# Sixty instead of fifty-six single-row gather tiles in a graph-attention layer

## Chip, cores and metric

One Trainium2 chip, one core of it. The metric is the device time of one execution in microseconds (us), median of three timed executions, lower is better. A profiled execution stands beside them; its trace gives every number that is not a timed one.

## What is computed

A graph layer over N = 6250 nodes and E = 206250 edges (sorted by receiver), 128 features in 8 heads of 16, all float32:

```
w   = silu(edge_feats @ rad_W1 + rad_b1) @ rad_W2 + rad_b2
    + silu(chi_scalar @ sph_W1 + sph_b1) @ sph_W2 + sph_b2     # per edge
q   = (x @ Wq)[receivers];  k = (x @ Wk)[senders];  v = (x @ Wv)[senders]
alpha = (q * w * k).sum(head) / sqrt(16) * cutoffs             # 8 numbers per edge
out = segment_sum(alpha * v, receivers) / 16
return layernorm(x + out)
```

## The kernel before

**Stages.** A first stage (some 65 us) makes the table kv_tab in device memory: one row of 1 KB per node, k and v side by side. Then one long loop runs over the edges. 128 edges are a tile, four tiles a *quad*, four quads a *group*; there are 403 quads, taken in an order that swaps the two middle ones of a group. The loop has one *slot* per quad, and in slot i the engines are at different quads: TensorE (PE) makes the hidden layer of quad i+2 (L533), brings q to the edges of quad i+1 (L542) and weighs quad i+1 (L580); ScalarE (ACT) takes the two silus of quad i+2 (L563) and a copy out of PSUM; VectorE (DVE) multiplies quad i+1 by the k of its senders (L593) and ends quad i (L601 to L620: product, sum over heads, scale, messages). PE sums the messages by receiver with one-hot matrices (L632), and per group the totals are normalized and written (L690 to L749).

**How the sender rows come.** GpSimd (POOL) issues one indirect DMA per tile (L136, `gather`), 128 rows of kv_tab by the indices of the tile, into a ring of 16 quads. It is 14 quads ahead of the loop: the gathers of quad i+14 wait for the matmuls of quad i (`gathers`). The quads 0 to 7 need no gather (their rows are made from gathered x in the first stage).

**Single rows.** In 56 of the quads (`row_quads`) the fourth tile is not gathered. Its 128 rows are fetched by 128 plain DMAs of one row each (L203, `load_rows`), 64 issued by SyncE (SP) and 64 by ACT, into a buffer named wide. The row addresses are in a table at_i, and an engine loads them into its registers some at a time (`ROW_UNITS`; L198), before the issues. The places of these quads are `row_at`: evenly between ROW_FIRST and ROW_LAST. The issues for tile k are spread over the slots from row_at[k-1] - ROW_LEAD + 1 to row_at[k] - ROW_LEAD; in each slot SP's come at the end of its program for the slot, ACT's behind its second silu, but for two (ROW_CARRY) that are kept for the next slot and put one before and one behind the PSUM copy, between the two silus (`copies`, `next_rows`). In a row quad DVE's multiply and its messages are two instructions each, three tiles from kv and one from wide (`kv_parts`).

**The end.** The last quads 400 to 402 are summed without the receivers' 32-wide one-hots: three wide one-hots (L639 to L643 on DVE, `wide_one_hots`) are made in slots 392, 394 and 396 and scaled by ACT (L650, four instructions) in slots 393, 395 and 397. They share the three buffers named wide with the single-row tiles. The totals of four groups are kept in y0 (two buffers) until they are written.

**Order.** The order on each engine is the program's own (the schedule is by hand); what waits is in order behind what waits before it on its engine or queue.

Of the kernel before, what the change touches and what calls it, by code (L numbers as in the profile page):

```python
# [12 lines left out]
F32 = mybir.dt.float32  # L13
# [8 lines left out]
SP = mybir.EngineType.SP  # L22
ACT = mybir.EngineType.Activation
WAIT = mybir.DependencyInfo(mybir.DependencyClass.Sync, mybir.DependencyReason.DATA)

P = 128
N = 6250
D = 128
# [5 lines left out]
QT = 4  # L34
# [10 lines left out]
LB = 4  # L45
# [1 line left out]
XQ = 8  # L47
MSGS = 10
RING = 16
ROW_TILES = 56  # L50
ROW_FIRST = 20
ROW_LAST = 392
ROW_LEAD = 8
ROW_ACT = 64
ROW_CARRY = 2
ROW_UNITS = {SP: 32, ACT: 32}
XU = 4
WRITE_LAG = 3
READY_LAG = 2
# [10 lines left out]
def gnn_kernel(ctx, tc, x, src, dst, weight, edges, rad_W1, rad_b1, rad_W2, rad_b2,  # L70
# [26 lines left out]
    src_x = const.tile([P, math.ceil(XQ / NQ) * GT], I32, name="src_x")  # L97
    at_i = const.tile([ROW_TILES, P], I32, name="at_i")
    scale = const.tile([P, NT], F32, name="scale")
# [23 lines left out]
    gp = ctx.enter_context(tc.tile_pool(name="group", bufs=2))  # L123
# [8 lines left out]
    def quad_of(name, bufs, width=D):  # L132
        return ep.tile([P, QT, width], F32, name=name, bufs=bufs)
# [8 lines left out]
    order = [g * NQ + j for g in range(NG) for j in (0, 2, 1, 3) if g * NQ + j < QUADS]  # L142
    row_at = [ROW_FIRST + (n + 1) * (ROW_LAST - ROW_FIRST) // ROW_TILES for n in range(ROW_TILES)]
    row_quads = {order[i] for i in row_at}
# [22 lines left out]
    feats_of, relb_of, act_of, kv_of, hot_of, hotT_of, x_of, q_of, msg_of = ({} for _ in range(9))  # L167
    po_of, part_of, to_of, tot_of, xT_of, y0_of, kq_of, pick_of, pq_of, pw_of = ({} for _ in range(10))
# [16 lines left out]
    def load_rows(i):  # L185

        k = next((k for k in range(ROW_TILES) if i <= row_at[k] - ROW_LEAD), None)
        start = None if k is None else (row_at[k - 1] if k else ROW_FIRST) - ROW_LEAD + 1
        if k is None or i < start:
            return next_rows(ACT, owed[ACT])  # L190
        q = order[row_at[k]]
        slots = row_at[k] - ROW_LEAD + 1 - start
        table = kv_tab.bitcast(U8).rearrange("(o n) b -> o (n b)", o=1)

        def rows_by(engine, name, a, b):
            for e in range(a, b, ROW_UNITS[name]):
                m = min(ROW_UNITS[name], b - e)
                rows = nc.values_load_multi_w_load_instructions(  # L198
                    at_i[k:k + 1, e:e + m], engines=(name,), min_val=0,
                    max_val=(N - 1) * ROW_BYTES,  # L200
                    skip_runtime_bounds_check_because="senders are nodes")[1]
                for p, r in zip(range(e, e + m), rows):
                    yield lambda p=p, r=r: signalled(engine.dma_start(  # L203
                        row_of[q][p:p + 1, 0, :].bitcast(U8), table[:, ds(r, ROW_BYTES)]))
# [7 lines left out]

        n = P - ROW_ACT
        if i == start:
            row_of[q] = quad_of("wide", 3, P)[:, :2, :].rearrange("p t d -> p (t d)")[:, None, :]
            rows_left[SP].append(rows_by(nc.sync, SP, 0, n))
            rows_left[ACT].append(rows_by(nc.scalar, ACT, n, P))
        for engine, m in ((SP, n), (ACT, ROW_ACT)):
            a, b = (math.ceil(m * j / slots) for j in (i - start, i - start + 1))
# [99 lines left out]
    with tc.tile_pool(name="nodes", bufs=1) as nodes, \  # L319
# [76 lines left out]

        rows_f = nodes.tile([P, ROW_TILES], F32, name="rows_f")

# [6 lines left out]
        def turn_rows():  # L405
            pt = nps.tile([P, QT, P], F32, name="pt", bufs=3)
            nc.tensor.transpose(pt[:ROW_TILES, 0, :], rows_f, ident)
            nc.vector.tensor_copy(at_i, pt[:ROW_TILES, 0, :])

# [117 lines left out]
    with tc.tile_pool(name="ps", bufs=1, space=PSUM) as pp, tc.tile_pool(name="loop", bufs=1) as lp:  # L527
# [108 lines left out]
        def wide_one_hots(q):  # L636

            t = slice(q * QT, (q + 1) * QT)
            d = gp.tile([P, QT], F32, name="d", bufs=NQ)  # L639
            nc.vector.tensor_copy(d, dst_i[:, t])  # L640
            nc.vector.tensor_scalar(d, d, gb[:, q // NQ:q // NQ + 1], None, op0=OP.subtract)
            hot_of[q, "wide"] = quad_of("wide", 3, P)
            nc.vector.tensor_tensor(hot_of[q, "wide"], d[:, :, None].to_broadcast([P, QT, P]),  # L643
                                    colp[:, None, :].to_broadcast([P, QT, P]), op=OP.is_equal)

# [33 lines left out]
        def first_of(g):  # L679

            return max(g - (g - (NG - LB)) % LB, 0)

        def moments(g, total, adder=nc.vector, added=False):
            first = first_of(g)
            if g == first:
                y0_of[g] = (gp.tile([P, LB, D], F32, name="y0"), gp.tile([P, LB, 2], F32, name="mv"))
            y0, mv = y0_of[first]
            k = g - first
            if not added:
                adder.tensor_tensor(y0[:, k, :], total, x_of[g], op=OP.add)  # L690
            st = gp.tile([P, 6], F32, name="st")
            nc.vector.bn_stats(st, total if added else y0[:, k, :])
            nc.vector.bn_aggr(mv[:, k, :], st)
# [45 lines left out]
        def statistics(g):  # L739
            moments(g, tot_of[g])  # L740
            if g < NG - LB and first_of(g + 1) > g:
                inverse_roots(first_of(g), g + 1)
# [42 lines left out]
        for g in range(NG - 1):  # L785
            for slot, j in enumerate((0, 2, 1, 3)):
                q = g * NQ + j
# [56 lines left out]
                if g == NG - 3 and slot in (0, 2):  # L844
                    wide_one_hots(order[slot // 2 - 3])
                if g == NG - 2 and slot == 0:
                    wide_one_hots(order[-1])
                    n = nc.values_load(general, min_val=0, max_val=1)
                    place(g)
                    place(NG - 1)  # L850
# [34 lines left out]
        for t in range(QT):  # L885
            sum_wide(b, t)
        moments(g - 2, tot_of[g - 2], nc.gpsimd)
        multiply(c, mark)
        moments(g - 1, tot_of[g - 1], nc.gpsimd)
        sd = roots(g - 2, g)  # L890
        normalize(g - 2, g, sd)
# [10 lines left out]
        ys, mv = y0_of[first_of(g)]  # L902
# [162 lines left out]
```

## Time and profile before

| | us |
|---|---|
| timed executions | 1966.3, 1967.48, 1971.83 (median 1967.48) |
| profiled execution, its own time | 1966.43 |
| its span, first to last instruction | 1964.3 |
| mean granted PE clock | 0.942 |
| POOL busy | 1476.0 |
| PE busy | 1770.4 |
| DVE busy | 1516.8 |
| ACT busy (without its DMA issues and register loads) | 648.3 |
| gathers by POOL in the loop's ring | 1524 |
| single rows by SP, by ACT | 3584, 3584 |

A row of the waits names who waited, for what, the total in us, the number of waits and the longest. A row of the timeline has start, duration, engine, line, operation, result and sources, and in brackets the idle time of the engine before it and what ended it. A row of the windows has the stretch, its length, busy us and number of instructions, the granted PE clock, the busy share of the 16 DMA engines and GB/s. POOL's duration of a gather is the time to issue it; the rows land later.

### The profile page before, as it was taken

How to read it: one execution, taken by the hardware profiler on the slowest of the kernel's cores; microseconds unless marked ns; L12 is line 12 of the kernel's file. 1: busy time of each engine (PE TensorE's matmuls, PEld its weight loads, DVE VectorE, ACT ScalarE, POOL GpSimd, SP SyncE). 2: the span in 40 equal slices, each digit the busy share in tenths (PEclk: the TensorE clock that was granted, in tenths of full speed). 3: DMA queues.
4: the chain of work that ended last, by engine and by line, in shares of the span. 5: the costliest groups of instructions: out<-in, count | busy, mean ns of one | idle time of the engine just before them, and what ended most of it. 6: DMA issues, size and time to landing. Idle time of an engine off the chain costs nothing. (4 is left out here: it accounts for less than half of the span.)

```text
span 1964.3 us, 57621 instructions
## 1 busy us (share of the span) xinstructions
PE 1770.4 (90%) x15990; PEld 1480.0 (75%) x15990; DVE 1516.8 (77%) x3411; ACT 648.3 (33%) x1360; POOL 1476.0 (75%) x1566
## 2 busy tenths in 40 slices
PE   9899999799999888889999988989889988898898
PEld 7788777677877777777877777778777777777776
DVE  6788888688877687777787777877777777777787
ACT  3333333232433333332332333333323323333333
POOL 7777777777777777777777777777777777777775
PEclk9899999898989899989899899999998999999999
DMA  9555555555555555555555555555555555555553
GB/s 343 154 151 147 154 155 148 155 156 148 159 148 152 155 150 157 147 158 156 157 146 157 147 157 146 155 148 155 156 146 156 147 155 150 152 158 145 157 143 93
DMA packets 153253, 305.44 MB, mean 155 GB/s; under 512 B 40300, under 2 KB 87260, under 8 KB 152924
## 3 DMA queue, kind: packets, MB, share of 16 engines
q0 software_dynamic: 74176, 201.95, 36.7%
q1 hardware_dynamic: 70080, 95.67, 15.6%
q10 hardware_dynamic: 8668, 4.08, 1.0%
q8 instruction: 127, 2.08, 0.5%
q14 instruction: 202, 1.65, 0.3%
HBM read 288.10 MB, written 13.46 MB: 154 GB/s over the span
## 5 line engine op out<-in xcount | busy, mean ns | idle before, releaser
L136 POOL DMA_INDIRECT kv<-kv_tab,src_i x1524 | 1442.6, 947 | 465.0 <-issue 198.8
L563 ACT ACTIVATE act<-ph,b 128x512 f32<-128x512 f32 x806 | 553.3, 687 | 1259.5 <-PE pq L542 598.0
L580 PE MATMUL pw<-w,act 128*128 128x128 f32 x6448 | 881.4, 293 | 0.0
L580 PEld LDWEIGHTS pw<-w,act 128*128 128x128 f32 x6448 | 802.0, 203 | 96.3 <-issue 79.0
L533 PE MATMUL ph<-feats,w 32*128 32x512 f32 x1612 | 545.4, 670 | 58.5 <-ACT act L563 57.0
L542 PE MATMUL pq<-q,hotT 32*128 32x128 f32 x3224 | 487.6, 292 | 5.9 <-DVE kq L593 5.8
L593 DVE TENSOR_TENSOR kq<-pq,kv 128x512 f32<-128x512 f32 (+1 forms) x403 | 269.8, 669 | 249.1 <-DVEq L590 110.0
L542 PEld LDWEIGHTS pq<-q,hotT 32*128 32x128 f32 x3224 | 408.8, 195 | 19.7 <-DVE kq L593 15.5
L603 DVE TENSOR_REDUCE side<-kq 128x32 f32<-128x512 f32 x403 | 279.9, 695 | 43.6 <-DVE kq L601 1.4
L620 DVE TENSOR_TENSOR msg<-kv,side 128x512 f32<-128x512 f32 (+1 forms) x404 | 269.8, 668 | 43.5 <-PE pw L580 1.2
L533 PEld LDWEIGHTS ph<-feats,w 32*128 32x128 f32 x1612 | 154.0, 191 | 178.0 <-ACT act L563 115.6
L601 DVE TENSOR_TENSOR kq<-pw,kq 128x512 f32<-128x512 f32 x403 | 274.1, 680 | 0.6 <-PE pw L580 0.6
L575 PE MATMUL pw<-brow,onesb 3*128 3x512 bf16 x403 | 158.6, 393 | 0.6 <-DVE kq L601 0.6
L632 PE MATMUL po<-msg,hot 128*32 128x128 f32 x3200 | 156.6, 294 | 0.0
L673 PE MATMUL pq<-part,to 128*128 128x128 f32 x200 | 48.8, 330 | 95.6 <-DVE kq L593 93.2
L673 PEld LDWEIGHTS pq<-part,to 128*128 128x128 f32 x200 | 33.7, 212 | 105.1 <-DVE kq L593 90.2
L607 DVE TENSOR_TENSOR side<-side,scale 128x32 f32<-128x32 f32 x400 | 79.8, 200 | 42.3 <-DVE side L603 0.9
L632 PEld LDWEIGHTS po<-msg,hot 128*32 128x32 f32 x3200 | 73.1, 113 | 38.4 <-issue 4.6
L272 DVE TENSOR_TENSOR hotT<-relb,side 128x512 f32<-128x512 bf16 x101 | 68.7, 681 | 0.0
L277 DVE TENSOR_TENSOR hot<-rel,side 128x512 f32<-128x512 f32 x100 | 68.0, 680 | 0.0
L266 PE MATMUL pq<-wq,xT 128*128 128x128 f32 x200 | 41.6, 290 | 17.9 <-DVE kq L593 17.6
L690 DVE TENSOR_TENSOR y<-tot,x 128x128 f32<-128x128 f32 x98 | 28.2, 287 | 27.3 <-DMA out<-y 27.3
(121 smaller groups left out, 831.9 us busy)
## 6 DMA issues: line engine op xcount, KB each, us to landing
wide<-kv_tab SPq DMA_DIRECT2D x3584, 1.0 KB
wide<-kv_tab ACTq DMA_DIRECT2D x3584, 1.0 KB
feats<-in_edges SPq DMA_DIRECT2D x101, 512.0 KB
kv<-kv_tab,src_i POOLq DMA_INDIRECT x1524
relb<-rel_lin SPq DMA_DIRECT2D x101, 128.0 KB
x<-in_x SPq DMA_DIRECT2D x101, 64.0 KB
out<-y SPq DMA_DIRECT2D x101, 64.0 KB
kv_tab<-kv SPq DMA_DIRECT2D x12, 512.0 KB
```

Of the source, the lines that this page charges most:

```text
L136: return nc.gpsimd.indirect_dma_start(out=o, out_offset=None, in_=table, in_offset=bass.IndirectOffsetOnAxis(ap=index, axis=0))
L533: return nc.tensor.matmul(act_of[q, i], w1[r0:r0 + R, :], feats_of[g][r0:r0 + R, c0:c0 + EQ], start=True, stop=True)
L542: o = nc.tensor.matmul(pq_of[q][:, t, :], hotT_of[g][b, t * P:(t + 1) * P], q_of[g][b, :], start=True, stop=True)
L563: o = nc.scalar.activation(act, act_of[q, i], AF.Silu, bias=b1[:, i:i + 1])
L575: nc.tensor.matmul(pw, onesb, brow.rearrange("p t d -> p (t d)"), start=True, stop=False)
L580: o = nc.tensor.matmul(pw[:, t, :], act_of[q, i][:, t * P:(t + 1) * P], w2[:, i, :], start=False, stop=(t == QT - 1 and i == 1))
L593: o = nc.vector.tensor_tensor(kq_of[q][:, u, :], pq_of[q][:, u, :], kv[:, :, :D], op=OP.mult)
L601: nc.vector.tensor_tensor(m, pw_of[q][:, t, :], m, op=OP.mult)
L603: o = nc.vector.tensor_reduce(alpha, m.rearrange("p t (h e) -> p t h e", e=HD), AX.X, OP.add)
L620: o = nc.vector.tensor_tensor(msg_of[q][:, u, :].rearrange("p t (h e) -> p t h e", e=HD), kv[:, :, D:].rearrange("p t (h e) -> p t h e", e ...
L632: o = nc.tensor.matmul(po_of[g][j * W:(j + 1) * W, :], hot_of[g][:, j * QT + t, :], msg_of[g * NQ + j][:, t, :], start=(t == 0), stop=(t = ...
L673: nc.tensor.matmul(ph[:, :D], to[:n, 0, :], part[:n, :], start=True, stop=(g == 0))
```

## The change

There are 60 single-row quads, spread from 4 to 401 instead of from 20 to 392; they come every 6.617 instead of every 6.643 slots, the first is quad 10 (before: 26), the last 401 (before: 392). ACT issues 68 and SP 60 of the 128 rows. The issues of a tile end 5 instead of 8 slots ahead of its quad. ACT loads 24 addresses at a time: three loads a tile (24, 24, 20) instead of two of 32; SP has two, of 32 and 28. The wide one-hots of the end get three buffers of their own, and y0 has three buffers instead of two, both in the space that the first stage leaves free.

```
-ROW_TILES = 56
-ROW_FIRST = 20
-ROW_LAST = 392
-ROW_LEAD = 8
-ROW_ACT = 64
+ROW_TILES = 60
+ROW_FIRST = 4
+ROW_LAST = 401
+ROW_LEAD = 5
+ROW_ACT = 68
 ROW_CARRY = 2
-ROW_UNITS = {SP: 32, ACT: 32}
+ROW_UNITS = {SP: 32, ACT: 24}
...
-            hot_of[q, "wide"] = quad_of("wide", 3, P)
+            hot_of[q, "wide"] = lp.tile([P, QT, P], F32, name="hots", bufs=3)
...
-                y0_of[g] = (gp.tile([P, LB, D], F32, name="y0"), gp.tile([P, LB, 2], F32, name="mv"))
+                y0_of[g] = (lp.tile([P, LB, D], F32, name="y0", bufs=3), gp.tile([P, LB, 2], F32, name="mv"))
```

## The prediction

> **What bounds the kernel now.** I began with the page: who is busy, and who does the same thing most often. Then the waits, POOL first.
>
> ```profile
> span 1964.3 us, 57621 instructions
> L136 POOL DMA_INDIRECT kv<-kv_tab,src_i x1524 | 1442.6, 947 | 465.0 <-issue 198.8
> ```
>
> ```profile
> POOL kv L136 <- issue: 198.8, 652, 0.3
> POOL kv L136 <- PE pw L580: 182.3, 597, 0.3
> DVE kq L593 <- DVEq L590: 110.0, 69, 4.0
> DVE y L690 <- DMA out<-y: 27.3, 6, 9.3
> ```
>
> POOL never waits longer than 0.3 us before a gather: that is the step from one gather to the next, not a wait, whatever engine it is put down to. So POOL issues without a pause from the first gather to the last, while DVE stands 69 times in front of L590, where it waits for rows. The ends of that row of gathers in the timeline, and what DVE does behind it:
>
> ```profile
> 44.25 0.95 POOL L136 DMA_INDIRECT kv<-kv_tab,src_i  x1 [0.30 <-issue]
> ...
> 1950.56 0.95 POOL L136 DMA_INDIRECT kv<-kv_tab,src_i  x1 [0.30 <-issue]
> ...
> 1953.60 0.69 DVE L593 TENSOR_TENSOR kq<-pq,kv 128x512 f32<-128x512 f32 x1 [0.69 <-DVEq L590]
> ```
>
> (1950.56 - 44.25) / 1523 = **1.2517 us a gather**, start to start. POOL is the bound of the long middle; a gather that is left out there is worth 1.25 us.
>
> **From gather to multiply.** POOL's end is not DVE's start: the rows must land. Counting back from the last gather, 40 belong to quads 393 to 402, three to row quad 392, 24 to 386 to 391; so the last gather of 385 starts 67 steps before 1950.56 and that of 384 70 steps. For 395 it is 28 steps and for 396 it is 24. On DVE quad 385 is known by its split multiply.
>
> ```profile
> 1863.07 0.95 POOL L136 DMA_INDIRECT kv<-kv_tab,src_i  x1 [0.30 <-DVE side L607]
> 1866.82 0.95 POOL L136 DMA_INDIRECT kv<-kv_tab,src_i  x1 [0.30 <-issue]
> 1870.99 0.69 DVE L593 TENSOR_TENSOR kq<-pq,kv 128x512 f32<-128x512 f32 x1 [1.09 <-DVEq L590]
> 1875.04 0.56 DVE L593 TENSOR_TENSOR kq<-pq,kv 128x384 f32<-128x384 f32 x1
> 1875.52 0.28 DVE L593 TENSOR_TENSOR kq<-pq,wide 128x128 f32<-128x128 f32 x1
> ...
> 1915.55 0.94 POOL L136 DMA_INDIRECT kv<-kv_tab,src_i  x1 [0.30 <-issue]
> 1918.49 0.69 DVE L593 TENSOR_TENSOR kq<-pq,kv 128x512 f32<-128x512 f32 x1 [0.28 <-DVEq L590]
> 1920.56 0.94 POOL L136 DMA_INDIRECT kv<-kv_tab,src_i  x1 [0.30 <-issue]
> 1923.54 0.69 DVE L593 TENSOR_TENSOR kq<-pq,kv 128x512 f32<-128x512 f32 x1
> ```
>
> From the end of the last gather to the multiply: 1870.99 - 1864.02 = **6.97 us** for quad 384, waiting for rows to the last; 7.27 for 385; but 1918.49 - 1916.49 = 2.00 for 395 and 1923.54 - 1921.50 = **2.04 us** for 396. What lies between is the end of the single rows:
>
> ```profile
> L203 ACTq DMA_DIRECT2D wide<-kv_tab x3584: 227/228/788, 123.4 to 1878.9; - x200
> ```
>
> ```profile
> 1000.00:1500.00 500.00, 73.21 (x121) 0.94 0.54 153
> 1900.00:1924.00 24.00, 3.98 (x7) 1.00 0.38 108
> ```
>
> The last is issued at 1878.9, and the DMA engines' share falls from 0.54 to 0.38. While single rows are on their way a gather needs 5 us longer to land. A constant lag costs nothing in a loop; but where it ends the loop gets 5 us back, and before, that happened in time: quads 386 to 396 ran faster than POOL's step.
>
> **The change, part by part.** *POOL.* Four gathers fewer, 4 x 1.2517 = 5.0 us, at its last gather. At quad 396 it is three (59 of 60 row quads lie at or before 394, against all 56): its last gather ends 3.75 us earlier, at 1917.75. Nothing holds POOL back: the rows of the waits say so, and the first row quad takes one gather from a start where it waits for none.
>
> *The end of the rows.* The issues now run to slot 396, so quad 396 has a lag like 384's, not like 396's: 1917.75 + 6.97 = 1924.72 against 1923.54: **+1.2 us**. Bounds for the lag: 2.04 (the rows don't matter: -3.75 in all) and 7.27 (+1.5). I take 6.97, the quad as far from the last issue. The 5 us come back only in quads 398 to 402, and there they find no taker:
>
> ```profile
> DVE st L692 <- PE ph L654: 0.9, 1, 0.9
> DVE kq L593 <- DVEq L590: 0.7, 1, 0.7
> DVE kq L601 <- PE pw L580: 0.6, 1, 0.6
> ```
>
> These are DVE's longest waits from 1924 to the end: 2.2 us of 37, and for rows 0.7. From quad 396 on DVE works through (wide one-hots, inverse roots, the tail), and its start sets the end.
>
> *DVE.* Quad 401 becomes a row quad in that tail: 0.56 + 0.28 - 0.69 = 0.15 us, for the multiply and for the messages, **+0.3**. The other three stand where DVE waits for rows: nothing (0.9 us if it did not). The four added address columns before the loop, by this row
>
> ```profile
> 57.88 2.43 DVE L402 TENSOR_SCALAR rows_f<-src_i 128x1 f32<-128x1 int32 x39
> ```
>
> cost 4 x 0.06 us, with quads in stock: nothing.
>
> *Buffers.* The third y0 buffer takes away the 27.3 us of waits for the writes of y. The waits of 500 to 1000 us have five of the six,
>
> ```profile
> DVE y L690 <- DMA out<-y: 18.0, 5, 7.4
> ```
>
> and none comes later; in the first half POOL leads by many quads, and it did not pause for them: 0 to the sum (-27.3 if DVE were the bound). The wide one-hots' own buffers cost no instruction.
>
> *SP and ACT.* Issues and register loads:
>
> ```profile
> L198 SPq TENSOR_LOAD <-at_i x112: 1897/2167/2525, 108.8 to 1851.1; - x112
> L198 ACTq TENSOR_LOAD <-at_i x112: 2135/2228/2491, 121.0 to 1862.0; - x112
> ...
> L290 SPq TENSOR_LOAD <-gb_i x26: 469/568/1176, 24.2 to 1878.8; - x26
> ```
>
> ```profile
> 218.18 0.69 ACT L563 ACTIVATE act<-ph,b 128x512 f32<-128x512 f32 x1
> 218.26 4.69 ACTq L203 DMA_DIRECT2D wide<-kv_tab  x7
> 223.05 0.69 ACT L563 ACTIVATE act<-ph,b 128x512 f32<-128x512 f32 x1 [4.18 <-PE pw L580]
> ...
> 223.88 2.30 ACTq L203 DMA_DIRECT2D wide<-kv_tab  x7
> 226.29 0.69 ACT L563 ACTIVATE act<-ph,b 128x512 f32<-128x512 f32 x1 [1.79 <-PE pw L580]
> ```
>
> Seven issues take 2.30 us, 0.32 each; with a load of 32 addresses among them 4.69. A load of 4 takes 0.568 (L290), of 32 2.228: 0.059 us an address, so 24 take 1.75 and 20 take 1.51. ACT per tile: before 64 x 0.32 + 2 x 2.23 = 24.9 us, after 68 x 0.32 + 2 x 1.75 + 1.51 = 26.8; per slot 3.75 and 4.05, **+0.30 us a slot**. SP falls from 24.8 to 23.4 a tile. What ACT's 0.30 does hangs on the pace the loop could hold without POOL:
>
> ```profile
> 76.00:97.00 21.00, 4.09 (x6) 1.00 0.56 171
> 174.00:320.00 146.00, 23.16 (x40) 0.99 0.54 153
> ```
>
> Without single rows six multiplies in 21.0 us: 3.5 a slot. With them 34 quads in 146 us (40 less six split ones): 4.3, while POOL was far ahead. POOL's own pace after the change is (4 x 6.617 - 1) x 1.2517 / 6.617 = 4.82. 4.3 + 0.30 stays below it; so ACT keeps up, with 0.2 us a slot in hand instead of 0.5, and a hiccup is caught up later. For that, and for ACT's slots 393 and 395, where issues now meet the scaling of the wide one-hots,
>
> ```profile
> 1913.51 1.65 ACT L650 ACTIVATE wide<-wide,ends,scale 128x128 f32<-128x128 f32 x4 [0.25 <-DVE wide L643]
> ```
>
> I estimate +1.5 us at quad 396, between 0 (all is caught up) and 5 (both 1.65 us and a slot's excess stay). The shorter lead (5 slots of 4.8 = 24 us from the issues' end) I price at nothing; without that cover, see the third rival.
>
> **Sum:** +1.2 + 0.3 + 1.5 = +3.0 on the profiled execution's own time of 1966.43: 1969.4. The median of the timed runs is 1.05 higher; on it, **1970.5 us**.
>
> [...]
>
> **The rivals.** *ACT becomes the bound* (slower). Point of decision: quad 2 is multiplied at 75.99:
>
> ```profile
> 75.99 0.69 DVE L593 TENSOR_TENSOR kq<-pq,kv 128x512 f32<-128x512 f32 x1
> ```
>
> The first tile's issues now lie in slots 0 to 5, which grow from 3.5 to some 4.9 us (4.5 of issues and loads, and the silus): +8 us. From there 394 slots must fit before 1924.7: (1924.7 - 76.0 - 8) / 394 = 4.67 us. Above this POOL's lead is never used up, and each 0.01 costs 3.9 us. For it: 4.3 + 0.30 = 4.6 at a granted clock of 0.99, and the loop's mean is 0.94; if PE ended every slot that would add 4.3 x (0.99 / 0.94 - 1) = 0.2. Three loads a tile, some between the two silus. Against: a load slot leaves PE idle, so part of the extra issues and of the slow clock hide there, and SP, which was as full as ACT, has less. At 4.75 it gives 31 us over the forecast, about 2001; the bounds are 1970 and 2035.
>
> *The saving arrives* (faster): the lag of 396 is 2, or the tail has slack. 1967.5 - 3.75 + 0.3 = 1964; with all four gathers 1962.5. For it: the waits for rows are real now. Against: the 7 us above.
>
> *Rows come too late* (slower): lead 5 instead of 8, three slots or 14 us less; if 1 us a tile of that were missing, with ACT near its bound, +15 us: 1985. Against: no wait of DVE longer than 4.0 now.
>
> **Chances.** Forecast 0.50 (own range 1966 to 1975), ACT bound 0.32, saving arrives 0.12, rows late 0.06. Range 1964 to 1995: it leaves out half of the faster case and the dearer third of ACT's. About 0.3%, 5.9 us, is what a measurement can tell from no change: faster by more 0.03, within 0.55, slower by more 0.42.
>
> **What would show it.** POOL with 1520 gathers 1.25 us apart and no wait over 0.3; the last ends near 1946.5. Multiply of 396 about 7 us behind its last gather, that of 402 more than 4. DVE's waits for y gone. Slot pace of 4.5 to 4.65 early on, and waits at L590 in the second half; if these are missing and POOL waits for PE, the first rival holds. Wrong I am also if the lag at 396 is 2, or if DVE is idle in the tail.

## The result, and the profile after

The changed kernel takes 1976.6 us (median of 11 runs, 1968.57 to 1983.21), the kernel before on the same chip 1967.32 (11 runs, 1965.42 to 1971.83): ratio 1.0045, 95% interval 1.0029 to 1.0061. Forecast were 1970.5 us and a range of 1964 to 1995. On a second chip it was 1972.69 against 1966.96: 1.0039 (1.0024 to 1.0054). It is slower by some 6 to 9 us, though POOL has four gathers fewer.

The profiled execution's own time is 1971.17 us, 4.7 more than the one before. It is one of the shorter ones: what it shows explains those 4.7 us, not the whole of the median. The page first, two groups:

```profile
span 1969.3 us, 58686 instructions
...
L136 POOL DMA_INDIRECT kv<-kv_tab,src_i x1520 | 1438.1, 946 | 463.7 <-issue 186.5
L563 ACT ACTIVATE act<-ph,b 128x512 f32<-128x512 f32 x806 | 553.4, 687 | 1262.5 <-PE pw L580 756.6
```

Then the waits (total, number, longest):

```profile
ACT act L563 <- PE pw L580: 756.6, 270, 5.0
ACT act L563 <- PE pq L542: 315.5, 125, 7.1
DVE kq L593 <- PE pq L542: 235.9, 196, 6.2
PEld ph L533 <- ACT act L563: 219.1, 296, 2.5
POOL kv L136 <- issue: 186.5, 611, 0.3
POOL kv L136 <- PE pw L580: 183.3, 601, 0.3
...
DVE kq L593 <- DVEq L590: 19.2, 12, 3.6
```

POOL still issues without a pause: no wait is over 0.3 us. But DVE now waits for rows only 12 times (before 69), and for PE's q 196 times (before 72). TensorE's hidden layer, which before waited 115.6 us for the silus, waits 219.1. The rows before, for these two:

```profile
PEld ph L533 <- ACT act L563: 115.6, 169, 2.5
DVE kq L593 <- PE pq L542: 83.1, 72, 6.4
```

The row of waits for the writes of y is gone. So for most of the loop the slots set the pace, and POOL's lead lies idle. TensorE is busy for 92% of the span (before 90%); whether ACT lengthens the slots or TensorE fills them by itself, these rows do not settle. From the timeline, DVE's multiplies of quads 7, 348, 396 and 402, POOL's last gather of 396 (1916.27) and its last of all:

```profile
101.92 0.69 DVE L593 TENSOR_TENSOR kq<-pq,kv 128x512 f32<-128x512 f32 x1 [0.73 <-PE pq L542]
...
1695.18 0.56 DVE L593 TENSOR_TENSOR kq<-pq,kv 128x384 f32<-128x384 f32 x1 [1.22 <-PE pq L542]
...
1916.27 0.94 POOL L136 DMA_INDIRECT kv<-kv_tab,src_i  x1 [0.30 <-issue]
...
1927.47 0.69 DVE L593 TENSOR_TENSOR kq<-pq,kv 128x512 f32<-128x512 f32 x1 [0.52 <-DVEq L590]
...
1945.03 0.95 POOL L136 DMA_INDIRECT kv<-kv_tab,src_i  x1 [0.30 <-PE pw L580]
...
1956.96 0.69 DVE L593 TENSOR_TENSOR kq<-pq,kv 128x512 f32<-128x512 f32 x1
```

Three things are to be read here.

- **The middle.** (1695.18 - 101.92) / 341 = 4.672 us a slot, against POOL's 4.82. From a gather's end to its multiply there are 55 us at quads 8 to 24, 35 at quad 180, 22 at 240, 9.4 at 348: the lead shrinks by 0.15 a slot, and POOL ends the slots only for the last 50. Before, the same lag was 10 at quad 125.
- **The end of the rows.** Quad 396's last gather ends at 1917.21, 4.3 us earlier than before; its multiply starts 10.26 us later, 0.2 us after the rows have landed. It is 3.93 us later than before. DVE had stood idle for only 0.52 us ahead of it, since quads 394 and 395 had waited for their rows too (0.29 and 2.29 us).
- **The end.** From the multiply of 396 to that of 402 there are 29.49 us (before 30.06), from there to the end of the span 12.3 (before 10.7). 3.93 - 0.57 + 1.61 = 5.0, the difference of the spans.

The 1.6 us behind the last multiply are not DVE's. Its last operation and the last write, after:

```profile
1962.96 0.41 DVE L905 TENSOR_SCALAR y<-ph,mv,rs 128x128 f32<-128x128 f32 x1
1964.69 0.34 SPq L906 DMA_DIRECT2D out<-y  x1
```

DVE gets there in 6.0 us from 402's multiply (before 6.65). SP issues the last write 1.3 us after DVE's end (before 0.03), and the span ends 4.6 us after that issue (before 3.6). Why SP is late there, no row tells.

### The profile page after: what moved, and what is told of

It is laid out like the page before. It is cut to its first block, busy times and chain, and to the rows that moved or that the text cites. A ratio compares the mean times of both kernels' runs of the same rounds, so it can differ in the third digit from the quotient of the medians.

```text
span 1969.3 us, 58686 instructions
## 1 busy us (share of the span) xinstructions
PE 1815.7 (92%) x15990; PEld 1502.9 (76%) x15990; DVE 1519.7 (77%) x3423; ACT 652.6 (33%) x1360; POOL 1470.7 (75%) x1562
## 5 line engine op out<-in xcount | busy, mean ns | idle before, releaser
L580 PE MATMUL pw<-w,act 128*128 128x128 f32 x6448 | 894.7, 296 | 0.0
L580 PEld LDWEIGHTS pw<-w,act 128*128 128x128 f32 x6448 | 814.4, 205 | 90.7 <-issue 68.0
L533 PE MATMUL ph<-feats,w 32*128 32x512 f32 x1612 | 616.0, 663 | 107.5 <-ACT act L563 103.1
L533 PEld LDWEIGHTS ph<-feats,w 32*128 32x128 f32 x1612 | 179.8, 188 | 274.8 <-ACT act L563 219.1
L601 DVE TENSOR_TENSOR kq<-pw,kq 128x512 f32<-128x512 f32 x403 | 274.3, 681 | 0.0
L632 PE MATMUL po<-msg,hot 128*32 128x128 f32 x3200 | 152.6, 287 | 0.0
L673 PE MATMUL pq<-part,to 128*128 128x128 f32 x200 | 43.0, 299 | 26.9 <-DVE kq L593 26.8
L711 ACT ACTIVATE y<-y,shift,rs 128x128 f32<-128x128 f32 x100 | 48.2, 482 | 0.5 <-DVE shift L705 0.5
```

The lines of the kernel that those rows point to most:

```text
L533: return nc.tensor.matmul(act_of[q, i], w1[r0:r0 + R, :], feats_of[g][r0:r0 + R, c0:c0 + EQ], start=True, stop=True)
L580: o = nc.tensor.matmul(pw[:, t, :], act_of[q, i][:, t * P:(t + 1) * P], w2[:, i, :], start=False, stop=(t == QT - 1 and i == 1))
L601: nc.vector.tensor_tensor(m, pw_of[q][:, t, :], m, op=OP.mult)
L632: o = nc.tensor.matmul(po_of[g][j * W:(j + 1) * W, :], hot_of[g][:, j * QT + t, :], msg_of[g * NQ + j][:, t, :], start=(t == 0), stop=(t = ...
```

## The experiments

Of the five sets of runs only one got a chip on which the kernel before takes about 1967 us; on the chips of the other four it took 2625 to 2668 us itself, so a figure is compared only within its set. The sets are told in the order of what they decide, and the steady pace of the middle goes by the multiplies of quads 60 and 350.

### At 1967 us: the change again, ACT as before, the buffers alone

All three on one chip; the kernel before 1966.96 us (23 runs, 1964.77 to 1967.56).

**The change, unaltered.**

> The changed kernel itself, unaltered, beside the kernel before. Theory (the price of ACT's slots: four more issues and a third address load a tile use up the lead that POOL needs): where the kernel before takes about 1967 us, 1972 to 1980, ratio 1.002 to 1.007, and the single execution varies more than that of before because the quad at which POOL takes over moves. Where the kernel before takes about 2650 us, POOL is not the bound and ACT's four extra rows count in every slot: with eight extra rows costing 0.6 us a slot there, four cost 0.1 to 0.3 us a slot, so 2700 to 2800. Rival (the end of the rows alone, at slot 396, costs the time): 1970 in the first case, 2673 to 2680 in the second, no different from the versions with 64 rows by ACT.

Measured: 1972.69 us (1969.95 to 1981.49), 1.0039 (1.0024 to 1.0054); profiled execution 1970.76. Pace 4.68. The multiply of 396:

```profile
1927.86 0.69 DVE L593 TENSOR_TENSOR kq<-pq,kv 128x512 f32<-128x512 f32 x1 [2.10 <-DVEq L590]
```

10.3 us behind its last gather, as in the first profile. The time is at the low end of what the theory expected.

**64 rows by ACT in two loads, the rest of the change kept.**

```
-ROW_ACT = 68
+ROW_ACT = 64
-ROW_UNITS = {SP: 32, ACT: 24}
+ROW_UNITS = {SP: 32, ACT: 32}
```

> The changed kernel with ROW_ACT 64 and loads of 32 on both queues, so 64 rows and two loads a tile by ACT as before; everything else of the change stays. Theory (ACT's slots): where the kernel before takes about 1967 us, the pace of the slots from quad 7 to 200 falls from 4.67 to 4.5 or 4.6, POOL takes over by quad 200 to 250 and the time is 1968 to 1972, 3 to 6 us under the changed kernel; where it takes about 2650 us, 20 us or more under the changed kernel. Rival (end of the rows alone): within 2 us of the changed kernel in the same call. Second rival (the saving arrives once ACT is not in the way): 1963 to 1964.

Measured: 1970.75 us (1967.86 to 1973.80), 1.0020 (1.0010 to 1.0029); profiled 1969.41. The time fits the theory (1968 to 1972), and it fits the first rival as well: it is 1.94 us under the change, and the end of the rows alone allowed 2. The pace is not the theory's: 4.71, no faster than the change's 4.68, and POOL takes over no earlier. The waits:

```profile
ACT act L563 <- PE pw L580: 583.0, 195, 5.5
...
DVE kq L593 <- PE pq L542: 159.6, 149, 5.8
PEld ph L533 <- ACT act L563: 140.2, 201, 2.2
...
DVE kq L593 <- DVEq L590: 92.8, 28, 6.8
```

PE waits less for the silus (140.2 us, against 220.0 in the unaltered change), DVE less for PE's q (159.6 against 223.1), and another wait comes in their place. L590 is DVE's wait for rows, of both kinds. In 19 of the 28 the quad is a row quad whose gathers landed 2 to 38 us earlier, so it is the single rows that are late: 75.5 us in all. The longest, at quad 136, in the timeline:

```profile
700.88 0.56 DVE L593 TENSOR_TENSOR kq<-pq,kv 128x384 f32<-128x384 f32 x1 [6.83 <-DVEq L590]
```

and in the chain of work the pieces ahead of it (start, length, what):

```profile
684.51 0.03 SPq L203
684.54 0.03 issue
684.57 15.64 DMA wide<-kv_tab
...
700.88 0.77 DVE kq L593 x2
```

A row that SP issues at 684.5 lands 15.6 us later, and the multiply waits for it. The chain has twelve more such pieces, of 12.8 to 17.3 us each, ahead of late row quads between 63 and 314; eleven begin with an issue by SP, one with one by ACT. SP has 64 rows here and 60 in the change. The unaltered change has only four such waits in this set (8.7 us), and the first profile has none. SP's last row of a tile is issued 15.6 us before the tile's multiply here (median of the tiles), 22.7 in the change, and 36.4 and 33.0 in the kernel before and the one below, which have the lead of 8 slots, 64 rows by SP and no late row. So with 64 rows by SP the lead of 5 slots is too short. Without the 75.5 us the pace would be at most 75.5 / 290 = 0.26 lower: 4.45.

It is tempting to say that ACT's slots and SP's late rows bring the two versions to the same pace by two ways. That is not shown. Quads 26 to 60 of the five profiles have no wait at L590, and a quad's gathers end 18 us or more ahead of its multiply (us a slot; TensorE's busy time in it, and what is left; granted clock):

| | slot | TensorE busy | left | clock |
|---|---|---|---|---|
| before | 4.33 | 4.05 | 0.28 | 0.99 |
| before, buffers of the change (below) | 4.44 | 4.22 | 0.22 | 0.94 |
| change, first profile | 4.57 | 4.25 | 0.32 | 0.96 |
| change, this set | 4.64 | 4.29 | 0.34 | 0.95 |
| 64 rows by ACT | 4.62 | 4.32 | 0.30 | 0.93 |

With ACT's share undone the slot is hardly shorter than in the change: 4.62, or 4.54 without two waits, 2.8 us in all, that end just behind the landing of a row. From quad 7 to 26 it is shorter, 4.50 against 4.69 and 4.67. The two kernels with the rows of before differ by 0.11 between themselves, so 0.1 us can't be told in 34 slots. In all five TensorE is busy for 93 to 95% of the slot. That it sets the slots' pace, at the clock that it is granted, is a rival that no run at 1967 us tested.

What stayed as expected is the start, quad 7 at 97.72 instead of 101.4, and the end of the rows:

```profile
97.72 0.69 DVE L593 TENSOR_TENSOR kq<-pq,kv 128x512 f32<-128x512 f32 x1
...
1926.49 0.69 DVE L593 TENSOR_TENSOR kq<-pq,kv 128x512 f32<-128x512 f32 x1 [2.06 <-DVEq L590]
...
1955.69 0.69 DVE L593 TENSOR_TENSOR kq<-pq,kv 128x512 f32<-128x512 f32 x1
```

396 is 9.74 us behind its last gather, and 402 another 29.2 us behind it.

**The kernel before with the buffers of the change.**

```
-            hot_of[q, "wide"] = quad_of("wide", 3, P)
+            hot_of[q, "wide"] = lp.tile([P, QT, P], F32, name="hots", bufs=3)
...
-                y0_of[g] = (gp.tile([P, LB, D], F32, name="y0"), gp.tile([P, LB, 2], F32, name="mv"))
+                y0_of[g] = (lp.tile([P, LB, D], F32, name="y0", bufs=3), gp.tile([P, LB, 2], F32, name="mv"))
```

> The kernel before with the buffers of the change alone (the wide one-hots and a third y0 in the loop's space); rows, lead and loads as before. Theory: POOL issues without pause whatever DVE waits for, so where the kernel before takes about 1967 us the 27 us of waits for the writes of y go and the time stays within 1 us (ratio 0.9995 to 1.0005). Rival (the waits for y are on the path, since quads late in the first half are late for good): 5 to 27 us faster. Where the kernel before takes about 2650 us the slots are the bound, and a wait for y counts in full: 0 to 60 us faster, 60 being the gap of the two versions with half of TensorE's weigh.

Measured: 1965.68 us (1964.31 to 1967.16), 0.9996 (0.9987 to 1.0005): no difference that can be told. The waits, and the timeline:

```profile
DVE kq L593 <- DVEq L590: 139.1, 81, 3.9
```

```profile
94.02 0.68 DVE L593 TENSOR_TENSOR kq<-pq,kv 128x512 f32<-128x512 f32 x1
...
1920.08 0.95 POOL L136 DMA_INDIRECT kv<-kv_tab,src_i  x1 [0.30 <-issue]
...
1923.05 0.69 DVE L593 TENSOR_TENSOR kq<-pq,kv 128x512 f32<-128x512 f32 x1
...
1953.03 0.69 DVE L593 TENSOR_TENSOR kq<-pq,kv 128x512 f32<-128x512 f32 x1 [0.58 <-DVEq L590]
```

The 27.3 us of waits for y are gone, and DVE waits longer for gathers instead (139.1 us, before 110.0): the wait has only moved to the engine that bounds. This run is also the measure of the slots without POOL's bound and without y: quads 26 to 100 take 4.46 us each while the lag falls from 35 to 9, at a granted clock of 0.96. And with the rows ending at quad 392, quad 396 is multiplied 2.0 us behind its last gather. The version with 64 rows by ACT has the same buffers and the same number of rows by each queue, and its last gather of 396 ends 4.3 us earlier; yet its multiply of 396 starts 3.4 us later than here.

### At 2650 us: what these chips are

The same code ran in a different balance there. Two stretches of the windows (stretch, length, DVE busy at L601 and its number, granted PE clock, DMA share, GB/s), of the changed kernel's first profile:

```profile
500.00:1000.00 500.00, 72.83 (x107) 0.94 0.54 152
```

and of the version with the start undone (below):

```profile
500.00:1000.00 500.00, 54.45 (x80) 0.83 0.39 115
```

80 quads instead of 107 in 500 us. And the waits of the latter:

```profile
ACT act L563 <- PE pw L580: 1249.6, 305, 8.2
DVE kq L593 <- PE pw L580: 601.8, 235, 4.8
POOL kv L136 <- PE pw L580: 485.9, 253, 22.9
```

POOL waits up to 22.9 us for TensorE's release of a buffer, so it isn't the bound; rows of the gathers lie ready some 80 us before their multiply. If a slot grew in inverse proportion to the granted clock, 0.83 instead of 0.94 would make 4.68 into 5.3 (an estimate), not 6.3. One more thing is slower: SP's step from one row's issue to the next is 0.52 us in the mean with 64 rows by each queue (0.35 in the same version at 1967 us), while ACT's is 0.35 in both. What else is slower there, the profiles do not tell. A quad's gathers land 1.8 us behind POOL's last, although 128 single rows come in every tile as well.

**Half of the weigh left out of both kernels,** to take the load off TensorE.

```
-                for i in range(2):
-                    o = nc.tensor.matmul(pw[:, t, :], act_of[q, i][:, t * P:(t + 1) * P], w2[:, i, :],
-                                         start=False, stop=(t == QT - 1 and i == 1))
-                    marks.append(o)
+                o = nc.tensor.matmul(pw[:, t, :], act_of[q, 0][:, t * P:(t + 1) * P], w2[:, 0, :],
+                                     start=False, stop=(t == QT - 1))
+                marks.append(o)
```

> The kernel before with half of the edge weights' second layer left out (the spherical half: four of eight matmuls of L580 a quad), so that PE has less to do and a low granted clock weighs less; the output is not the reference's. Rows, gathers, silus and issues are as before. Every theory: if PE's slots fall below POOL's 4.82 us, POOL is the bound as in the first profile and the time is 1960 to 1975 whatever the clock; if PE still ends the slots, more than 2050. It is the base for the same cut of the changed kernel.

> The changed kernel with the same half of the second layer left out. Theory A (ScalarE's issues and loads set the pace): ScalarE's work is not touched by the cut, 4.05 us of issues and loads a slot and some 0.5 of silus and copies, so the pace stays at 4.5 to 4.7, POOL's lead lasts to quad 250 or beyond, and it is 2 to 20 us over the same cut of the kernel before. Theory B (the end alone costs 9 us): the lead is used up by quad 150 as before, and it is 6 to 10 us over. Theory P (PE, not ScalarE, set the pace of 4.67): PE is lighter, so the lead is used up by quad 150 and the time is within 3 us of the same cut of before.

Measured: the kernel before so lightened 2681.31 us, 1.0057 (1.0035 to 1.0080) of the whole kernel before, 2668.03; the changed one 2621.43, 0.982 (0.9792 to 0.9849). All expectations for the changed one missed: it is 60 us under the other, not over. Half of the weigh is worth next to nothing there. That doesn't clear TensorE as what fills the 6.3 us, since the granted clock fell to 0.65 and 0.63, and TensorE was busy for 76 and 82% of the span, against 82% in the version with the start undone, which weighs in full. The 60 us between the two have a row in the first,

```profile
DVE y L689 <- DMA out<-y: 140.1, 16, 14.0
```

and none in the second, which has the third y0 buffer. It fits that a wait for y counts where the slots are the bound, and not where POOL is (27.3 us of such waits gone at 1967 us, the time the same). That it is the buffer alone was not run on these chips.

### At 2650 us: parts of the change

First set, one chip, the kernel before 2662.88 us: 64 rows by ACT; 68 rows, but 59 tiles up to quad 394; 76 rows by ACT; 64 rows and 59 tiles up to 394. The second set repeats the first of these on another chip (before 2625.09).

```
-ROW_ACT = 68
-ROW_UNITS = {SP: 32, ACT: 24}
+ROW_ACT = 64
+ROW_UNITS = {SP: 32, ACT: 32}
```

> The changed kernel with ScalarE's share undone alone: 64 rows by each engine, loads of 32 addresses, two a tile; the 60 places, the lead and the buffers stay. Theory A (ScalarE's issues and loads set the slot pace of about 4.67 us): ScalarE's sum falls from 26.8 to 24.9 us a tile, the pace from quad 7 on to 4.4 to 4.55, POOL's lead is used up by quad 250, VectorE waits for rows again in the second half, and only the end's price stays: 1968 to 1971, with executions that differ by less than 4 us. Theory B (the end alone costs the 9 us: rows to slot 396): no change, 1974 to 1979. Theory C (the lead of 5 slots makes the row copies late): no change or slower, 1976 to 1985, since SyncE has more to issue.

```
-ROW_TILES = 60
-ROW_LAST = 401
+ROW_TILES = 59
+ROW_LAST = 394
```

> The changed kernel without its last row tile: 59 tiles from 4 to 394 at the same spacing, so that the issues end at slot 389 instead of 396; one gather more. Theory A: the pace up to quad 390 stays at 4.6 to 4.7, but in slots 390 to 396 ScalarE is free and PE can run at 3.6 to 4 us a slot, and gathers land in 2 us: 4 to 7 us less than the changed kernel, 1970 to 1973, the spread of the executions stays. Theory B: the end was the whole cost, so it falls below the kernel before by the 3 gathers: 1963 to 1965. Theory C: no change, 1974 to 1979.

```
-ROW_ACT = 68
-ROW_UNITS = {SP: 32, ACT: 24}
+ROW_ACT = 76
+ROW_UNITS = {SP: 32, ACT: 26}
```

> A dose of the suspected cost: the changed kernel with 76 rows by ScalarE (three loads of 26, 26 and 24 addresses) and 52 by SyncE. Theory A: ScalarE's sum rises by 8 x 0.32 + 0.5 = 3.1 us a tile, 0.46 us a slot, over some 390 slots up to 180 us; where PE or POOL still ends some slots less, so 2080 to 2160, with POOL held back by TensorE's marks (waits over 0.3 us), since the loop's pace passes POOL's 4.82. Theories B and C: SyncE has less to do and the end is the same: 1970 to 1980.

The fourth joins the first two edits.

> Both undone: 64 rows by each engine in loads of 32, and 59 tiles from 4 to 394. Theory A with the landing lag: POOL is the bound up to quad 396 and three gathers are saved (3.75 us), the lag is back at 2 us before the tail: 1963 to 1965, faster than the kernel before. If the lead of 8 slots were needed, or the tail absorbs it: 1967 to 1970. Theory B: the same as the run without the last tile alone.

> The changed kernel with ScalarE's share undone alone (64 rows by each engine, two loads of 32 a tile), once more, where PE's granted clock is like that of the first profiles (0.94). Theory A (ScalarE's issues and loads set the pace of 4.67 us a slot): pace 4.4 to 4.55 from quad 7 on, POOL's lead used up by quad 250, 1968 to 1971 where the kernel before has 1967. Theory B (the end alone): 1974 to 1979. Theory C (the lead of 5 slots is too short): 1976 to 1985. If PE's clock is granted at 0.82 again, PE ends the slots and none of the three can be told: within 1 per cent of the kernel before.

| | us | ratio to before (95%) | pace, us a slot | waits for single rows, quads 60 to 350 |
|---|---|---|---|---|
| 64 by ACT | 2678.21 | 1.0048 (1.0030 to 1.0066) | 6.39 | 57.5 us |
| the same, second chip | 2635.53 | 1.0045 (1.0025 to 1.0064) | 6.28 | 33.9 |
| 68, to 394 | 2672.91 | 1.0030 (1.0015 to 1.0045) | 6.39 | none |
| 64, to 394 | 2676.61 | 1.0062 (1.0039 to 1.0085) | 6.36 | 38.3 |
| 76 by ACT | 2909.16 | 1.0924 (1.0901 to 1.0946) | 6.95 | none |

What these were to tell, whether the end of the rows or ACT costs the few us at 1967, they could not: multiplies lie 60 to 80 us behind their gathers, so the end of the rows hides. With 64 rows by each queue the single rows come late here too, in the version with 68 and 60 up to quad 394 they don't, and the pace is nearly the same. But 68 and 60 are no safeguard: the changed kernel with half of the weigh left out has them, at a pace of 6.23, and DVE waits 46.6 us for single rows by the measure of the table. The largest row of such waits, of the whole run (its lines are numbered one lower):

```profile
DVE kq L592 <- DVEq L589: 42.1, 7, 8.0
```

The eight rows more by ACT make a slot 0.56 us longer (6.95 - 6.39). In that version ACT's silu waits for nothing but ACT's own queue 612.0 us, in the 68-row version 157.9; first 76, then 68, each with ACT's loads of addresses (number, then shortest, middle and longest in ns):

```profile
ACT act L563 <- issue: 612.0, 94, 9.7
L198 ACTq TENSOR_LOAD <-at_i x180: 1677/2192/6150, 131.2 to 2861.9; - x180
```

```profile
ACT act L563 <- issue: 157.9, 69, 4.7
L198 ACTq TENSOR_LOAD <-at_i x177: 15/1719/1983, 131.0 to 2604.6; - x177
```

The 0.56 is no price of the eight rows, though the prediction's prices give 8 x 0.32 + 8 x 0.059 = 3.0 us a tile, 0.46 a slot. The second of the three loads of a tile, of 26 addresses, takes 5.99 us there (median), the first, also of 26, 2.19; in the 68-row version that second load, of 24, takes 1.81. All three are 10.0 us a tile against 5.1, and with the eight issues ACT has 7.5 us more a tile, 1.1 a slot. About half of it shows in the slots. So enough work on ACT's queue does lengthen the slots, but not in full, and most of this dose came from one load whose length no row explains.

### At 2650 us: start undone, end undone

The version with 64 rows by ACT, with the rows from quad 20 on as before (57 tiles), and with the rows up to quad 392 as before (58 tiles).

```
-ROW_TILES = 60
-ROW_FIRST = 4
+ROW_TILES = 57
+ROW_FIRST = 20
```

> The version with 64 rows by ACT and loads of 32, with the start undone as well: 57 row quads over 20 to 401, so the end of the rows stays at slot 396 and a gather fewer than before. Where the kernel before takes about 1967 us: theory (the end of the rows costs: quad 396 is multiplied 8 to 10 us behind its last gather instead of 2): POOL takes over by quad 200, 396 is multiplied at 1927 to 1930 against 1923.5 before, 396 to 402 takes 29 to 30 us, time 1970 to 1973. Rival (the late start, 8 to 24 us at quads 7 to 50, is what costs): 1965.5 to 1967, since one gather of 1.25 us is saved and the start is that of before.

```
-ROW_TILES = 60
-ROW_LAST = 401
+ROW_TILES = 58
+ROW_LAST = 392
```

> The version with 64 rows by ACT and loads of 32, with the end undone as well: 58 row quads over 4 to 392, so rows start in the first slots as in the change, end at slot 387, and two gathers fewer than before. Where the kernel before takes about 1967 us: theory (the end costs): the lag of 396 is back at 2 to 4 us, 396 is multiplied at 1921 to 1923, 2.5 us of gathers are kept, time 1964 to 1966. Rival (the late start costs, POOL's lead of 55 us is hardly used up at a slot pace of 4.67): the lag at quad 350 stays over 10 us and the time is 1969 to 1973.

Measured: 2657.81, 0.9979 (0.9961 to 0.9996), and 2663.18, 1.0003 (0.9981 to 1.0024), of 2662.89. Paces 6.33 and 6.32, waits for single rows 32.2 and 26.3 us. These do not answer the question, since the kernel before took 2663 us. Both have a row tile every 6.7 slots instead of 6.617 and less waiting for late rows, and both stand better than the 64-row version's 1.0045 to 1.0062; start and end can't be told apart here. A run of each at 1967 us is missing, and so are one of the third load alone and one of the lead alone.

## Why the prediction was right or wrong

The sign of the difference was right and the time lies in the range: +3.0 us was forecast, +9.3 and +5.7 were measured in the median and +4.7 in the profiled execution. On the first chip it is above the forecast's own 1966 to 1975, where the forecast and its first rival meet; on the second, 1972.69, it is inside. That the first falls within the range is owed to the range's width towards that rival, not to the sum. By its steps:

- **POOL: right.** 1520 gathers, no wait over 0.3, the last ends at 1945.98 (forecast 1946.5).
- **The end of the rows: right in mechanism, too small in size.** This is the term of the sum that was mis-sized. It was +1.2 us at quad 396, from a lag of 6.97. Measured are 10.26, 10.3 and 9.74 in the three profiles at 1967 us with rows to slot 396, against 2.0 in the two whose rows end at quad 392, and +3.9 us. Over quads 30 to 383 of the change the landing of a quad's gathers behind its last has a median of 7.3 and goes from 5.2 to 9.4 in 90 of 100; the prediction took one quad, 384, for a quantity that swings by 4 us, and the end hangs on one quad, 396. It is not mere chance either: 396 lands 10.1, 10.1 and 9.5 us behind in the three, and of the 354 quads of the change only 15 land more than 9.5 behind. Why that quad is among the slowest no row tells. This term gives the profiled execution's 3.9 of 4.7 us. The prediction's "While single rows are on their way a gather needs 5 us longer to land" held at 1967 us, and by more than 5: 396 lags 10 us with rows about and 2.0 without. It does not hold at 2650 us: 128 rows come in every tile there too, and the landing is 1.8 us behind. Which of the DMA engines move the rows, and whether that makes the lag, no row shows.
- **The four gathers find no taker at the end: right.** DVE waits 0.5 us for rows at quad 396 and not at all behind it, and 402 lags 11 us. The tail was to cost +0.3 and had -0.6 up to 402's multiply, and +1.6 behind it, of which nothing had been foreseen.
- **Buffers: right.** The buffers alone are worth nothing that can be measured (1965.68 us against 1966.96, ratio 0.9987 to 1.0005).
- **Start: right.** +8 us at quad 7 was said, 7.9 measured (101.92 against 94.0). But the slots from 7 to 50 lose another 16 us to before, since the first row quad is 10 and no longer 26; this was not in the sum.
- **The lead: the price held, its reason did not.** The prediction counted 5 slots, 24 us, from the end of a tile's issues to its use. But quad p is multiplied in slot p - 1, so it is three to four slots: in the first profile ACT's last row of a tile is issued 12.9 us before the multiply, and the last row lands 4.4 us before it (medians of the tiles, for the landing without the last eight; before 29.0 and 20.0). In the change that is enough but for 8.7 us of waits in one of two profiles; with 64 rows by SP it is not.
- **ACT and the slots: this step failed.** The prediction put "4.3 + 0.30 stays below it; so ACT keeps up, with 0.2 us a slot in hand", and +1.5 us at quad 396. The 4.3 was read from a stretch at a granted clock of 0.99; with the same rows at 0.94 the slots took 4.44 (buffers alone, quads 26 to 60). The change took 4.57 and 4.64 there and 4.69 and 4.68 from 60 to 350, so that 4.6 came out of a base too low. What was added is 0.13 to 0.2, and that it is ACT's is not shown, since undoing ACT's share took hardly any of it back. ACT's own sum was right: its three loads took 1.72, 1.81 and 1.55 us, 5.1 a tile where 5.0 were said. In hand were 0.15 us a slot, not 0.2, and the lead to use up was 55 - 7 = 48 us. 48 / 0.15 = 320 slots: from quad 24 that is quad 344; measured 348. In the profiled executions this comes just in time, and little or nothing of it is left at 396. The first rival's point of decision, 4.67 us from slot 7 on, is the pace that was measured, 4.672, so the forecast's own case held by next to nothing.

**What stays argued.** The end of the rows alone fits the profiled executions and the version with 64 rows by ACT (3.8 us over before). What the change's median has beyond that, some 2 us on one chip and 5 on the other, has no run that shows its cause. Other executions of the change are up to 12 us longer than its profiled one (1983.21 against 1971.17). At 3.9 us for each 0.01 of pace, 0.05 us a slot more than measured (0.02 until the lead isn't used up by quad 396, and 0.03 beyond) gives those 12 us, and with it the median. It fits that versions in which POOL takes over by quad 150 spread over 3 us in the one set at 1967 us (the kernel before, the buffers alone), the version with late rows over 6 and the change over 11.5; but in the first measurement the kernel before spread over 6.4 us as well. A long execution was not profiled, so this is not shown. Of ACT's 1.9 us more a tile, 0.6 are the loads and 1.3 the four issues; which of them the slots feel was not run. The rival of rows too late was priced at 1985 with a chance of 0.06: in the change itself rows are hardly ever late, but with 64 rows by each of the two queues they are, by 75 us of waits at the lead of 5. The rival in which the saving arrives (1962.5 to 1964) was not seen in any run.

## What to carry to other kernels

When work is taken off the engine that bounds, look at the pace of the next one over a long stretch and with the granted clock of that stretch: here 0.15 us a slot was the whole room, and the changed slots used it up. Two engines that share a stream of transfers have to be weighed together: with four rows moved back from ACT to SP, SP's rows came late (75.5 us of waits, 8.7 before that) and the pace stayed (4.71 us a slot, 4.68 before that). Count a lead from the last issue to the instruction that uses the data, not in nominal slots: 24 us on paper were 12.9 on ACT's queue. And look whether a saving in the middle of a pipeline reaches its end: here POOL's last gather of quad 396 ended 4.3 us earlier, but with rows issued up to slot 396 the multiply came 10.26 us behind that gather instead of 2.04, and 3.93 us later than before.

## What the runs showed of the hardware

- With 128 single rows in 6.617 slots of 4.67 us (4.1 a us) a quad's gathers landed 7.3 us behind POOL's issue of the last, at the median; with 128 in 6.617 slots of 6.3 us (3.1 a us), at 2650 us, it was 1.8, the same as with no rows at all at 1967 us (1.8 for quads 395 and 396 of the kernel before). That the rate of the single rows makes the difference is not shown: the gathers are a quarter rarer at 6.3 us too, and the chip is another.
- With half of the weigh left out the granted clock was lower, 0.647 and 0.627, where the other runs at 2650 us had 0.78 to 0.83; TensorE stayed busy for 76 and 82% of the span, and the time of the kernel before did not fall with the work (2681.31 us, 2668.03 whole).
- A load of 26 addresses into ACT's registers took 2.19 us as the first of a tile and 5.99 as the second (medians of 60 tiles, 76 rows by ACT); the first two of a tile took 1.72 and 1.81 with 24 addresses, 2.20 and 2.25 with 32 (medians, the change and the kernel before at 1967 us).
- Waits for writes of y of 27.3 us cost nothing that could be measured at 1967 us (1965.68 without them, 1966.96 with them); in the lightened kernel at 2681 us they came to 140.1 us. In the version with 64 rows by ACT POOL never waited over 0.3 us before a gather at 1970.75 us, and up to 23.0 us for TensorE at 2678.21 us: the same code on two chips.
